# A selective scan's slots reordered: decays half a slot earlier, due work first, one step of dt a slot, and the scan's first state read as a column operand

## The chip, the cores and the metric

The kernel runs on one NeuronCore of one Trainium2 chip. The metric is the device time of that core in microseconds (us). The kernel before took 5128.9 us in the median of three runs (5122.36 to 5136.76 us). Only one core is used, so nothing waits for another core.

Five engines take part, each with its own queue that it works off strictly in order: TensorE (PE in the profile), VectorE (DVE), ScalarE (ACT), GpSimd (POOL), and SyncE (SP), which here only issues DMAs. An instruction that waits for a semaphore holds up everything behind it on its own queue.

## The reference, cut to what matters

The program is a network of four layers on two sequences (B = 2) of 1024 positions and 1024 features. The change touches only the attention half of layer 2, a selective state-space block, here shortened:

```
proj = hidden_states @ in_proj_w             # 1024 -> 2 x 2048
x, z = split(proj); x = silu(causal_conv4(x))
ssm_p = einsum('bdl,ed->ble', x, x_proj_w)   # 64 + 16 + 16 values per position
dt_r, B, C = rmsnorm of the three parts
dt = softplus(dt_r @ dt_proj_w + dt_bias)
A = -exp(A_log)
# for every channel d (2048) and state n (16), over the positions t:
h[t] = exp(dt[t] * A) * h[t-1] + dt[t] * B[t] * x[t]
y[t] = sum over n of h[t] * C[t]
out = ((y + D * x) * silu(z)) @ out_proj_w
```

## The kernel before, in words

`l2_attn(b, ...)` (from L1061) is called once for each of the two sequences, b = 0 and 1. A sequence is cut into two halves of 512 positions, u = 0 and 1 (`HALF` = 512), and the 2048 channels into 16 chunks c of 128. The second half begins where the first ended, so the last state of half 0 must reach half 1.

**A slot.** The recurrence runs in 2 * SL = 256 slots k for each sequence, 128 for each half, eight for each chunk. `of(k)` turns a slot into (u, c, q, jj). A slot holds 2 x 128 rows, a row being one channel with one state, so it has two scans, m = 0 and 1, of 128 x 512. For slot k the program issues:

- `rows(k)`, six slots early: a DMA that reads dt * x of 16 channels back from DRAM (`dxd`), each repeated for its 16 states, into a tile `h` (128 x 1024, nine buffers). L1273.
- `times_b(k)`, two slots early: GpSimd multiplies h by B. L1279.
- `decay(k, m)`: TensorE spreads dt over the states (`rep` times `hl`, L1286) into a PSUM tile, and ScalarE makes exp(A * dt) of it in place (L1288). There are eight PSUM tiles of 128 x 512 for everything, handed out as they come free.
- in half 1 only, also in `decay`: ScalarE works on one column, h[:, 0] += exp(A dt)[:, 0] * hst (L1291), so that the kept state `hst` of half 0 enters.
- `scan(k, m)`: VectorE's `tensor_tensor_scan`, decay times state plus input, with initial value 0.0. L1296.
- `keep(k)`, one slot late, in half 0 only: ScalarE copies the last column of both scans into `hst`. L1304.
- `times_c(k)`, one slot late: VectorE multiplies both scans' results by C. L1307.
- `states(k)`, in odd slots: TensorE sums over the states with `sel` into y (L1318), and once a chunk adds D * x (L1316).

**The order is written out by hand** (`manual_schedule`): the loop at the end of `l2_attn` fixes each engine's order. Into the slots it weaves other work of the block: two matmuls a slot from a list `todo` (the next half's input projection L1349, the gate's L1403, the output projection L1441), and a table `late` of work that is due in a given slot, filled by `at(k, f)`. In slot k the order is: issue rows, times_b, keep(k-1); first matmul; scan(k,0), decay(k+1,0); the due work; second matmul; scan(k,1), decay(k+1,1); states, times_c(k-1).

**Due work.** For each chunk, 16 slots ahead, `l2_dt(u, c, k)` makes dt: a matmul in slot k (L1211), then in slot k+1 three ScalarE operations (Relu, Abs, Exp: L1221 to L1223), in k+2 three more (L1226 to L1228), in k+3 two GpSimd operations (L1231, L1232), in k+4 one (L1235), in k+5 the product with x (L1238) and its four DMAs to `dxd` (L1240), in k+7 a ScalarE rounding copy into `hl` and GpSimd's remainder (L1247, L1252), in k+8 the remainder's two DMAs (L1258). x is loaded in slot k+3 (L1520's list, tile `xi`, two buffers). Other due work: the convolution for half 1 (`l2_x` on ScalarE, `l2_taps` on VectorE L1124, `l2_silu` on ScalarE L1129 with its DMA to `xcd` L1130), the gate's silu (`silu_z`, L1388; each silu costs a load of the activation table before and one after, L193), the normalisation of ssm_p (`l2_norm`, `l2_spread`), and `y_out`: ScalarE copies y out of PSUM (L1332), GpSimd multiplies it by the gate (L1333), a DMA sends it to `yd` (L1334).

The tiles `e`, `one`, `lg` and `rl` of the dt work have one buffer each; `dtx`, the product with x, uses the tile `e`, and `y_out` uses the tag `one`.

Of the kernel before, what the change touches and what calls it, by code (L numbers as in the profile page):

```python
# [27 lines left out]
class Net:  # L28
# [1032 lines left out]
    def l2_attn(self, b, ready, last):  # L1061
# [4 lines left out]
        with (  # L1066
# [56 lines left out]
                for k in range(1, 4):  # L1123
                    nc.vector.scalar_tensor_tensor(p, xp[:, k : k + HALF], cw[:, c, k : k + 1], p, ALU.mult, ALU.add)  # L1124

            def l2_silu(u, c, p):
                acc = tmp("xo")
                self.other = True
                nc.scalar.activation(acc, p, AF.Silu)  # L1129
                nc.sync.dma_start(xcd[u][c][:], acc)  # L1130
                return acc

            def l2_px(u, c, acc):
# [24 lines left out]
                    elif c % 4 < 3:  # L1158
                        quarter[-1](c % 4 - 1)

            def l2_norm(u):
# [9 lines left out]
                nc.scalar.activation(pn, p[:, : 4 * NF], AF.Square)  # L1171
                ss = self.small([P, 4, 3], "ss")
# [14 lines left out]
                return pnv  # L1187
# [20 lines left out]
            def l2_dt(u, c, k):  # L1208

                p = self.ps()  # L1210
                nc.tensor.matmul(  # L1211
                    p, wd[c // 8][: NF + 1, (c % 8) * P : (c % 8 + 1) * P], norms[u][0], start=True, stop=True
                )
                xs[u, c] = xc = tmp("xi")
                at(k + 3, nc.sync.dma_start, xc, xcd[u][c][:])
                e, one, lg = tmp("e", 1), tmp("one", 1), tmp("lg", 1)
                dt, dtx = lg, e
                rl = tmp("rl", 1)

                def act1():  # L1220
                    nc.scalar.activation(rl, p, AF.Relu)  # L1221
                    nc.scalar.activation(e, p, AF.Abs)
                    nc.scalar.activation(e, e, AF.Exp, scale=-1.0)  # L1223

                def act2():
                    nc.scalar.activation(one, e, AF.Identity, bias=self.one)  # L1226
                    nc.scalar.activation(lg, one, AF.Ln)
                    nc.scalar.activation(one, one, AF.Identity, bias=neg)  # L1228

                def pool1():  # L1230
                    nc.gpsimd.tensor_tensor(e, e, one, ALU.subtract)  # L1231
                    nc.gpsimd.tensor_tensor(lg, lg, e, ALU.add)  # L1232

                def sum1():
                    nc.gpsimd.tensor_tensor(dt, lg, rl, ALU.add)  # L1235

                def times_x():
                    nc.gpsimd.tensor_tensor(dtx, dt, xc, ALU.mult)  # L1238
                    for j in range(4):
                        nc.sync.dma_start(dxd[u][c][:, j, :], dtx[32 * j : 32 * j + 32, :])  # L1240

                low = [None]

                def parts():

                    hl[u, c] = tp.tile([P, 2, HALF], R, tag="hl", bufs=2, name=self.nm("hl"))
                    nc.scalar.copy(hl[u, c], dt.unsqueeze(1).to_broadcast([P, 2, HALF]))  # L1247

                def rest():

                    lo = low[0] = tp.tile([P, HALF], R, tag="lo", bufs=1, name=self.nm("lo"))
                    nc.gpsimd.tensor_tensor(lo, dt, hl[u, c][:, 0, :].bitcast(F), ALU.subtract)  # L1252

                def send():

                    lo = low[0]
                    for j in range(2):
                        nc.sync.dma_start(  # L1258
                            hl[u, c][64 - 64 * j : P - 64 * j, j, :].bitcast(F), lo[64 * j : 64 * j + 64, :].bitcast(F)
                        )  # L1260

                for n, f in ((1, act1), (2, act2), (3, pool1), (4, sum1), (5, times_x), (7, parts), (7, rest), (8, send)):
                    at(k + n, f)


# [17 lines left out]
            def decay(k, m):  # L1283
                u, c, q, jj = of(k)
                dA[k, m] = self.ps()
                nc.tensor.matmul(dA[k, m], rep[:, 4 * m + q, :], hl[u, c][:, jj, :], start=True, stop=True)  # L1286
                g = 16 * c + 4 * q + 2 * jj + m
                nc.scalar.activation(dA[k, m], dA[k, m], AF.Exp, scale=A[:, g : g + 1])  # L1288
                if u:
                    h0 = hs[k][:, m, 0:1]  # L1290
                    nc.scalar.activation(h0, dA[k, m][:, 0:1], AF.Identity, scale=hst[:, g : g + 1], bias=h0)  # L1291

            def scan(k, m):
                u, c, q, jj = of(k)
                g = 16 * c + 4 * q + 2 * jj + m
                nc.vector.tensor_tensor_scan(  # L1296
                    hs[k][:, m, :], dA.pop((k, m)), hs[k][:, m, :], 0.0, ALU.mult, ALU.add
                )

            def keep(k):  # L1300
# [27 lines left out]
            def y_out(k):  # L1328
                u, c = k // SL, k % SL // 8
                sz = zt.pop((u, c))  # L1330
                yo = tmp("one", 1)
                nc.scalar.copy(yo, py.pop((u, c)))  # L1332
                nc.gpsimd.tensor_tensor(sz, sz, yo, ALU.mult)  # L1333
                nc.sync.dma_start(yd[u][c][:], sz)  # L1334

            def ins(u):

                def one(u, c):
# [6 lines left out]
                    def call(k, now):  # L1345
                        if k == 0:
                            w["p"] = self.ps()
                        p = w["p"]
                        nc.tensor.matmul(  # L1349
                            p, w["w"][:, k * P : (k + 1) * P], self.xcols(k, u0, HALF), start=k == 0, stop=k == KD - 1  # L1350
                        )
                        if k == KD - 1:
                            def x():
                                w["x"] = l2_x(u, c, p)
                            at(now + 1, x)
                            at(now + 2, lambda: l2_taps(c, p, w["x"]))

                            def s():
                                w["s"] = l2_silu(u, c, p)
# [5 lines left out]
            def xproj(u):  # L1365

                def one(c2):
# [7 lines left out]
                    def call(n, now):  # L1375
                        l2_px(u, 2 * c2 + n, w["x"][:, n * HALF : (n + 1) * HALF])
                        if 2 * c2 + n == NCH - 1:
                            at(now + 1, lambda: at(now + 3, l2_spread, u, l2_norm(u)))
# [83 lines left out]
            with self.tc.manual_schedule():  # L1462
# [12 lines left out]
                take(xproj(1), 4)  # L1475
                take(z0[12:] + z1[:6], 20)
                taken = 0
                at(-BEFORE, lambda: at(4 - BEFORE, l2_spread, 0, l2_norm(0)))
                for k in range(-BEFORE, 2 * SL + 6):
                    if -16 <= k < 2 * SL - 16 and k % 8 == 0:  # L1480
                        l2_dt((k + 16) // SL, (k + 16) % SL // 8, k)
# [26 lines left out]
                        times_b(k + 2)  # L1508
                    if 0 <= k - 1 < 2 * SL:
                        keep(k - 1)  # L1510
                    pe()
                    for m in range(2):
                        if live:
                            scan(k, m)
                        if 0 <= k + 1 < 2 * SL:
                            decay(k + 1, m)
                        if m:
                            break
                        for f, args in late.pop(k, []):
                            f(*args)  # L1520
                        pe(True)
                    if k % 2 == 1 and 0 <= k - 2 < 2 * SL:
                        states(k - 2)
                    if 0 <= k - 1 < 2 * SL:
                        times_c(k - 1)
                    if live and k % 8 == 4:
                        at(k + 8, y_out, k)
                    if live and k % 8 == 0:
                        skip(k // SL, k % SL // 8)
                while late:  # L1530
# [462 lines left out]
```

## Time and profile before

| what | value |
|---|---|
| median of three runs | 5128.9 us |
| the profiled execution | 5130.32 us |
| its span, first to last instruction | 5128.4 us |
| granted TensorE clock, mean | 0.968 |
| instructions | 50257 |
| VectorE scans (L1296) | 1024, 1207 ns each, 1204.1 us |
| VectorE times_c (L1307) | 512, 1193 ns each, 610.8 us |
| GpSimd times_b (L1279) | 512, 2367 ns each, 1201.0 us |
| ScalarE exp of the decay (L1288) | 1024, 657 ns each, 667.9 us |
| ScalarE column operation (L1291) | 512, 352 ns each, 180.0 us |

The profiled execution took 5130.32 us, 1.9 us more than its span and 1.4 us more than the median of the runs; sums are made against 5130.3. The page gives each engine's busy time, a picture of the span in 40 slices of 128 us (a digit is the busy share in tenths), and groups of instructions by line, with the idle time of the engine just before them and what ended it. The waits give the same by pairs, the timeline lists instructions in order, and the busy time of a stretch is given by windows. Lines of VectorE that follow each other without a wait overlap a little: two scans together take 2.33 us, not 2.41.

### The profile page before, as it was taken

The numbers are of one execution on the slowest core, as the hardware profiler recorded it, in microseconds if no ns is written. First come the engines' busy times: TensorE is split into PE (matmuls) and PEld (weight loads), VectorE is DVE, ScalarE is ACT, GpSimd is POOL, SyncE is SP. The second block draws the span as 40 slices with busy tenths as digits, with TensorE's granted clock in tenths as the row PEclk, the third lists the DMA queues.
The fourth block names the chain that finished last, engine by engine and source line by source line (L and its number), as shares of the span: only waits on it lengthen the run. The fifth ranks groups of instructions, "written<-read, shape, count | busy, mean of one in ns | idle before, by whom it ended". The sixth has DMA issues, their size and how long they took to land. (4 is left out here: it accounts for less than half of the span.)

```text
span 5128.4 us, 50257 instructions
## 1 busy us (share of the span) xinstructions
PE 4706.3 (92%) x16584; PEld 2237.2 (44%) x16584; DVE 3128.0 (61%) x4322; ACT 2109.7 (41%) x4485; POOL 2097.7 (41%) x1259
## 2 busy tenths in 40 slices
PE   8989989998897888999999999899888988899999
PEld 3347645433332333455433576554333333344544
DVE  5453256389999997225365422652899999963153
ACT  2431232377677774001024311424776777720010
POOL 2013121078798885100020220200887998831010
PEclk9999999999999999999999999999999999999999
DMA  2144212388889998201111432113888899971100
GB/s 88 36 159 143 97 48 81 131 216 217 220 225 242 236 244 226 90 33 46 49 67 38 173 119 89 54 51 103 220 219 224 214 247 245 249 210 65 55 20 33
DMA packets 254871, 708.06 MB, mean 138 GB/s; under 512 B 37008, under 2 KB 54544, under 8 KB 254612
## 3 DMA queue, kind: packets, MB, share of 16 engines
q1 hardware_dynamic: 248340, 683.88, 46.7%
q0 software_dynamic: 6272, 20.98, 1.2%
q8 instruction: 133, 2.18, 0.2%
q14 instruction: 126, 1.03, 0.1%
HBM read 599.60 MB, written 86.25 MB: 134 GB/s over the span
## 5 line engine op out<-in xcount | busy, mean ns | idle before, releaser
L1296 DVE TENSOR_TENSOR_SCAN h<-ps,h 128x512 f32<-128x512 f32 x1024 | 1204.1, 1207 | 88.9 <-ACT h L1291 47.2
L1279 POOL TENSOR_TENSOR h<-h,br 128x1024 f32<-128x1024 f32 x512 | 1201.0, 2367 | 43.3 <-DMA h<-dxd 20.7
L1286 PE MATMUL ps<-hl,rep 128*128 128x512 f32 x1024 | 717.9, 708 | 119.9 <-DVE h L1296 94.7
L1288 ACT ACTIVATE ps<-ps,l_Alog 128x512 f32<-128x512 f32 x1024 | 667.9, 657 | 216.9 <-PE ps L1286 213.6
L1307 DVE TENSOR_TENSOR h<-h,ps 128x1024 f32<-128x1024 f32 x512 | 610.8, 1193 | 0.0
L1403 PE MATMUL ps<-xT,w 128*128 128x512 f32 x1024 | 541.1, 615 | 10.2 <-DVE h L1296 7.9
L1608 POOL TENSOR_TENSOR x<-x,row 128x1024 f32<-128x1024 f32 x48 | 112.3, 2349 | 796.0 <-PE ps L130 796.0
L1286 PEld LDWEIGHTS ps<-hl,rep 128*128 128x128 f32 x1024 | 198.6, 195 | 523.6 <-DVE h L1296 340.1
L152 DVE TENSOR_TENSOR x<-x,ps 128x512 f32<-128x512 f32 x192 | 128.4, 681 | 434.4 <-PE ps L1785 145.6
L1318 PE MATMUL ps<-h,sel 128*32 128x512 f32 x2048 | 365.1, 638 | 18.8 <-DVE h L1307 18.2
L104 PE MATMUL ps<-xT,w 128*128 128x512 f32 x768 | 336.1, 592 | 0.0
L177 ACT ACTIVATE rs<-mv 128x1 f32<-128x1 f32 (+2 forms) x88 | 17.9, 203 | 705.7 <-DVE mv L171 705.4
L1441 PE MATMUL ps<-w,w 128*128 128x512 f32 x512 | 279.9, 630 | 20.8 <-DMA w<-yd 12.1
L1403 PEld LDWEIGHTS ps<-xT,w 128*128 128x128 f32 x1024 | 190.6, 195 | 204.2 <-issue 136.7
L104 PE MATMUL ps<-w,xT 128*128 128x512 f32 (+1 forms) x768 | 278.3, 522 | 0.0
L1124 DVE SCALAR_TENSOR_TENSOR ps<-xp,l_convw,ps 128x512 f32<-128x512 f32 x192 | 144.4, 752 | 213.4 <-ACT ps L1119 208.9
L767 POOL TENSOR_TENSOR s<-s,l1r 128x512 f32<-128x512 f32 x64 | 66.5, 1040 | 487.7 <-DVE l1r L766 481.8
L1349 PE MATMUL ps<-xT,w 128*128 128x512 f32 x512 | 251.9, 602 | 0.7
L1291 ACT ACTIVATE h<-ps,h,hst 128x1 f32<-128x1 f32 x512 | 180.0, 352 | 118.5 <-POOL h L1279 93.9
L1782 PE MATMUL ps<-w,xT 128*128 128x512 f32 x512 | 227.4, 597 | 0.0
L1622 PE MATMUL ps<-w,w 128*128 128x512 f32 x512 | 222.6, 594 | 4.2 <-DMA w<-yd 4.2
L104 PEld LDWEIGHTS ps<-xT,w 128*128 128x128 f32 x768 | 144.8, 189 | 183.4 <-issue 177.6
(289 smaller groups left out, 7319.9 us busy)
## 6 DMA issues: line engine op xcount, KB each, us to landing
h<-dxd SPq DMA_DIRECT2D x512, 512.0 KB, 7.2
w<-l_in SPq DMA_DIRECT2D x128, 512.0 KB, 6.7
w<-l_out SPq DMA_DIRECT2D x96, 512.0 KB, 6.2
w<-l_conv SPq DMA_DIRECT2D x54, 512.0 KB, 3.9
w<-cvd SPq DMA_DIRECT2D x36, 512.0 KB, 3.3
w<-l_fw SPq DMA_DIRECT2D x32, 512.0 KB, 4.4
xcd<-xo SPq DMA_DIRECT2D x64, 256.0 KB, 2.2
xi<-xcd SPq DMA_DIRECT2D x64, 256.0 KB, 5.4
```

What stands on the lines that cost most here:

```text
L104: self.nc.tensor.matmul(out, lhsT, rhs, start=j == 0, stop=j == n - 1)
L1279: nc.gpsimd.tensor_tensor(hs[k], hs[k], norms[of(k)[0]][1].unsqueeze(1).to_broadcast([P, 2, HALF]), ALU.mult)
L1286: nc.tensor.matmul(dA[k, m], rep[:, 4 * m + q, :], hl[u, c][:, jj, :], start=True, stop=True)
L1288: nc.scalar.activation(dA[k, m], dA[k, m], AF.Exp, scale=A[:, g : g + 1])
L1296: nc.vector.tensor_tensor_scan(hs[k][:, m, :], dA.pop((k, m)), hs[k][:, m, :], 0.0, ALU.mult, ALU.add)
L1307: nc.vector.tensor_tensor(hs[k], hs[k], norms[of(k)[0]][3].unsqueeze(1).to_broadcast([P, 2, HALF]), ALU.mult)
L1318: nc.tensor.matmul(py[u, c][32 * j : 32 * j + 32, :], self.sel[:, q, :], hs[k - 1 + j // 2][:, j % 2, :], start=False, stop=q == 3,)
L1349: nc.tensor.matmul(p, w["w"][:, k * P : (k + 1) * P], self.xcols(k, u0, HALF), start=k == 0, stop=k == KD - 1)
L1403: nc.tensor.matmul(p, w["w"][:, k * P : (k + 1) * P], self.xcols(k, u * HALF, HALF), start=k == 0, stop=k == KD - 1)
L1441: nc.tensor.matmul(p, y[:, cc, t * P : (t + 1) * P], wt[:, cc * HALF : (cc + 1) * HALF], start=c2 == 0 and cc == 0, stop=last,)
L1622: nc.tensor.matmul(acc[tt], y[:, cc * HALF + tt * P : cc * HALF + (tt + 1) * P], w[:, cc * HALF : (cc + 1) * HALF], start=c == 0, stop=c = ...
L1782: nc.tensor.matmul(p, self.xcols(k, tt * P, P), wt[k][:, ns], start=k == 0, stop=False)
```

## The change

The edits, all within `l2_attn`:

1. The column operation of ScalarE (L1291) is gone; in half 1 the scan takes the column of `hst` as its initial value instead of 0.0.
2. In slot k the decays issued are (k+1, 1) after the first scan and (k+2, 0) after the second, instead of (k+1, 0) and (k+1, 1).
3. The due work comes ahead of the slot's matmuls and scans, just behind keep(k-1), instead of behind the first scan.
4. dt's chain has one ScalarE operation a slot from the third on and one GpSimd operation a slot, and ends in slot k+10 instead of k+8. The DMAs of the product leave one slot after it, x is loaded one slot later, and the product uses the tile `one` instead of `e`.
5. `y_out` copies y one slot earlier, into a tile of its own, GpSimd multiplies two slots later and the DMA goes one slot after that.
6. The DMA of half 1's convolution result goes one slot later, and the normalisation is split over two slots.

```
@@ l2_silu
-                nc.sync.dma_start(xcd[u][c][:], acc)
+                if u:
+                    at(now + 1, nc.sync.dma_start, xcd[u][c][:], acc)
+                else:
+                    nc.sync.dma_start(xcd[u][c][:], acc)
@@ l2_dt
-                at(k + 3, nc.sync.dma_start, xc, xcd[u][c][:])
+                at(k + 4, nc.sync.dma_start, xc, xcd[u][c][:])
-                dt, dtx = lg, e
+                dt, dtx = lg, one
...
-                for n, f in ((1, act1), (2, act2), (3, pool1), (4, sum1), (5, times_x), (7, parts), (7, rest), (8, send)):
+                for n, f in (
+                    (1, act1), (2, act2), (3, act3), (4, act4), (5, act5), (5, pool1), (6, pool2), (7, sum1),
+                    (8, times_x), (8, parts), (9, send_x), (9, rest), (10, send),
+                ):
                     at(k + n, f)
@@ decay
                 nc.scalar.activation(dA[k, m], dA[k, m], AF.Exp, scale=A[:, g : g + 1])
-                if u:
-                    h0 = hs[k][:, m, 0:1]
-                    nc.scalar.activation(h0, dA[k, m][:, 0:1], AF.Identity, scale=hst[:, g : g + 1], bias=h0)
@@ scan
-                    hs[k][:, m, :], dA.pop((k, m)), hs[k][:, m, :], 0.0, ALU.mult, ALU.add
+                    hs[k][:, m, :], dA.pop((k, m)), hs[k][:, m, :], hst[:, g : g + 1] if u else 0.0, ALU.mult, ALU.add
@@ y_out
-                yo = tmp("one", 1)
+                yo = tmp("yo", 1)
                 nc.scalar.copy(yo, py.pop((u, c)))
-                nc.gpsimd.tensor_tensor(sz, sz, yo, ALU.mult)
-                nc.sync.dma_start(yd[u][c][:], sz)
+                at(k + 9, nc.gpsimd.tensor_tensor, sz, sz, yo, ALU.mult)
+                at(k + 10, nc.sync.dma_start, yd[u][c][:], sz)
@@ the loop over the slots
+                    for f, args in late.pop(k, []):
+                        f(*args)
                     pe()
                     for m in range(2):
                         if live:
                             scan(k, m)
-                        if 0 <= k + 1 < 2 * SL:
-                            decay(k + 1, m)
+                        if 0 <= k + 1 + m < 2 * SL:
+                            decay(k + 1 + m, 1 - m)
                         if m:
                             break
-                        for f, args in late.pop(k, []):
-                            f(*args)
                         pe(True)
...
-                        at(k + 8, y_out, k)
+                        at(k + 7, y_out, k)
```

The functions act1 to act5, pool1, pool2 and send_x are the old act1, act2, pool1 and times_x taken apart, with the same operations. In `l2_norm` the first part (copy, four transposes, squares) became `l2_norm1`, called in the slot in which the whole ran before; the rest and `l2_spread` come one slot later (for half 1; for half 0 all of it stays in one slot).

More of the change, by code (lines that the diff above doesn't have):

```diff
@@ L1124, in l2_taps, with l2_silu @@
                     nc.vector.scalar_tensor_tensor(p, xp[:, k : k + HALF], cw[:, c, k : k + 1], p, ALU.mult, ALU.add)
-            def l2_silu(u, c, p):
+            def l2_silu(u, c, p, now=0):
                 acc = tmp("xo")
@@ L1159, in l2_in, with l2_norm1 @@
                         quarter[-1](c % 4 - 1)
-            def l2_norm(u):
+            def l2_norm1(u):
                 raw = tmp("xo")
@@ L1171, in l2_norm @@
                 nc.scalar.activation(pn, p[:, : 4 * NF], AF.Square)
+                return p, pn
+            def l2_norm(u, p, pn):
                 ss = self.small([P, 4, 3], "ss")
@@ L1222, in act1, with act2, act3, act4 @@
                     nc.scalar.activation(e, p, AF.Abs)
+                def act2():
                     nc.scalar.activation(e, e, AF.Exp, scale=-1.0)
-                def act2():
+                def act3():
                     nc.scalar.activation(one, e, AF.Identity, bias=self.one)
+                def act4():
                     nc.scalar.activation(lg, one, AF.Ln)
+                def act5():
                     nc.scalar.activation(one, one, AF.Identity, bias=neg)
@@ L1231, in pool1, with pool2 @@
                     nc.gpsimd.tensor_tensor(e, e, one, ALU.subtract)
+                def pool2():
                     nc.gpsimd.tensor_tensor(lg, lg, e, ALU.add)
@@ L1238, in times_x, with send_x @@
                     nc.gpsimd.tensor_tensor(dtx, dt, xc, ALU.mult)
+                def send_x():
                     for j in range(4):
@@ L1358, in s @@
                             def s():
-                                w["s"] = l2_silu(u, c, p)
+                                w["s"] = l2_silu(u, c, p, now + 3)
                                 silu_z()
@@ L1377, in call @@
                         if 2 * c2 + n == NCH - 1:
-                            at(now + 1, lambda: at(now + 3, l2_spread, u, l2_norm(u)))
+                            at(now + 1, lambda: w.update(n=l2_norm1(u)))
+                            at(now + 2, lambda: at(now + 4, l2_spread, u, l2_norm(u, *w["n"])))
                     return load, [(call, n) for n in range(2)]
@@ L1477, in l2_attn @@
                 taken = 0
-                at(-BEFORE, lambda: at(4 - BEFORE, l2_spread, 0, l2_norm(0)))
+                at(-BEFORE, lambda: at(4 - BEFORE, l2_spread, 0, l2_norm(0, *l2_norm1(0))))
                 for k in range(-BEFORE, 2 * SL + 6):
```

## The prediction

> **What bounds the kernel now.** I read the page's slices first, then busy time by windows, then VectorE's waits, then the timeline at one wait.
>
> ```profile
> DVE  5453256389999997225365422652899999963153
> ```
>
> VectorE is full in two stretches of some seven slices: the slots of sequence 0 and of sequence 1. Elsewhere TensorE leads, and the change leaves that work alone. The windows cut the stretches at the first slot of half 1 (columns: length, then busy us of PE, PEld, DVE, ACT, POOL).
>
> ```profile
> 1052.00:1532.90 480.90, 425.52 (x1334) 161.82 (x1332) 459.42 (x434) 341.56 (x655) 415.45 (x224) 0.98 0.83 220
> 1532.90:2008.00 475.10, 401.55 (x1254) 149.56 (x1255) 448.25 (x407) 342.94 (x678) 403.04 (x214) 0.95 0.93 241
> 3601.00:4080.50 479.50, 426.63 (x1336) 162.52 (x1334) 459.40 (x434) 342.08 (x655) 415.37 (x224) 0.97 0.83 220
> 4080.50:4548.00 467.50, 401.35 (x1254) 148.13 (x1252) 445.89 (x404) 343.15 (x679) 403.37 (x214) 0.95 0.93 245
> ```
>
> VectorE is busy for 1813.0 of 1903.0 us; 90.0 us of idle time is all that a better order can win. The waits say what ends it (us, times, longest).
>
> ```profile
> DVE h L1296 <- ACT h L1291: 47.2, 63, 2.3
> ...
> DVE h L1296 <- ACT ps L1288: 31.4, 28, 5.7
> ```
>
> By windows, all 47.2 us of the first row lie in halves 1 (26.1 and 21.1) and all of the second in halves 0 (13.2 and 18.1). The timeline shows such a wait in half 0 on ScalarE:
>
> ```profile
> 1100.27 0.66 ACT L1288 ACTIVATE ps<-ps,l_Alog 128x512 f32<-128x512 f32 x1 [1.53 <-PE ps L1286]
> 1100.86 0.59 ACT L1332 COPY one<-ps 128x512 f32<-128x512 f32 x1
> 1101.46 1.28 ACT L1129 ACT_TABLE_LOAD   x1
> 1102.76 0.60 ACT L1129 ACTIVATE xo<-ps 128x512 f32<-128x512 f32 x1
> 1103.25 1.14 ACT L1388 ACTIVATE zo<-zo 128x512 f32<-128x512 f32 x2
> 1104.41 1.28 ACT L193 ACT_TABLE_LOAD   x1
> 1105.70 0.66 ACT L1288 ACTIVATE ps<-ps,l_Alog 128x512 f32<-128x512 f32 x1
> ```
>
> Between the slot's two exps stand 4.9 us of due work. The second scan of the next slot could start about 1104.1 and starts at 1106.40, 2.32 us late, behind the last line.
>
> **Part by part.**
>
> *Decays half a slot sooner, due work first (edits 2, 3).* The instructions stay the same. In the slot shown, due work could start behind keep at 1098.75; 4.9 us of it and one exp of 0.66 end at 1104.3, against a scan due at about 1104.1: 0.2 us late instead of 2.3. Most other bundles are smaller and leave nothing. Of the 31.4 us one 5.7 belongs to a sequence's first scan, which stays; 25.7 remain, of which I take 5 to stay: 20.7 won. An earlier decay holds its PSUM tile longer. The built program tells which tile each decay reuses: before, 196 of 1024 take the tile of a scan that only one further scan has followed (the decay's own scan is the third after it); after, 80 decays have that distance and the others more. So the tiles are no new limit.
>
> *No column operation (edit 1).* ScalarE loses 512 x 0.352 = 180 us; that alone is worth nothing, it is 72% busy here. What counts is the 47.2 us. Going through them scan by scan, 31.9 us fall on second scans, where due work lies between the exps (as above) and 0.35 us of column operation comes on top; 15.3 us fall on first scans, where ScalarE itself waited for GpSimd's times_b. Of the first kind I take 1 us to stay. Of the second, the scan now waits for GpSimd without 0.4 us of ScalarE between, and edits 4 and 5 take stalls from GpSimd; I take 6 to stay. Won: 40.2.
>
> Against this, 512 scans now read a column. No scan of the trace does. The nearest rows are two of VectorE's with one operation, shape and mixture of PSUM and SBUF, without and with a column (`rinv`):
>
> ```profile
> L1723 DVE SCALAR_TENSOR_TENSOR x<-ps,rinv,x 128x512 f32<-128x512 f32 x32 | 22.9, 746 | 9.0 <-PE ps L104 8.7 <-issue 0.3
> ...
> L628 DVE SCALAR_TENSOR_TENSOR qkv<-cf,ps 128x512 f32<-128x512 f32 x22 | 15.1, 686 | 69.4 <-PE ps L612 69.4
> ```
>
> 746 - 686 = 60 ns. The rows L266 (a column, 751) and L454 (a copy, 687) differ by 64. The Trainium skill, "VectorE: DVE Perf Modes", section "Scalar operands", puts a constant and a column side by side with no price; by it the edit is free. Its page "ScalarE: Activation LUTs", section "What ACT_TABLE_LOAD costs", counts about 93 ns for each column operand on ScalarE. The sums: 0, 512 x 0.060 = 30.7, or 47.6 us. I take 30.7, since the rows are of the same engine and the built program encodes the scan in that same instruction class. All of it is on the path: VectorE bounds half 1. This price eats half of what the waits give, so the halves 1 gain little.
>
> *dt one step a slot, GpSimd's gate later (edits 4, 5).* No operation is added. GpSimd has eight times_b of 2.367 and six products of 1.272 per chunk: 26.6 us, 3.32 a slot. VectorE without waits needs 3.36 (times_c 1.115, scans 1.133 and 1.112 from start to start) and 3.48 with columns. So GpSimd has little room, and its stalls matter: on batch 0 it waited 24.3 us for y's copy (L1333), 17.1 for x's load (L1238), 16.3 for `hl` (L1252). Each of these now has a slot more. They are off the path while GpSimd is ahead, and I count them only in the 9.3 us taken off first scans above.
>
> The DMAs move as well. The sends of the product leave SP's queue a slot after the product, so SP no longer stands on GpSimd (85.1 us on batch 0). But their landing comes closer to two readers. The first row load of the chunk is issued in the next slot instead of five later; from there to the first scan it has six slots, 20 us, against 7.2 for landing and 2.4 for times_b. And `one` is written again by the next chunk's act3 two slots after the sends, where `e` had four: ScalarE waits for the four landings, and exps and y's copy queue behind it. SP reaches slot 9's row load 1.4 us (median) after the slot's first scan, four issues take 1.7, landing 2.9 (median; 9.4 at most): 6.0 us, and ScalarE arrives at 6.7. Nothing typically; up to 6 us in a bad case. Of these 3.3 are covered: the next scan is due 5.5 us after keep, and keep, act3, y's copy and an exp take 0.2 + 0.7 + 0.6 + 0.7 = 2.2. I take 0; a gain is excluded, since a wait is only added.
>
> *Edit 6 and the start.* The longer chain must fit the 23 slots before the first scan. TensorE streams there without gaps, and ScalarE's loads of tables, not the chain, time it; the decay for slot 0 moves earlier, the product about 5 us later. I take 0, between -3 and +3 for each sequence.
>
> **Sum.** 5130.3 - 20.7 - 40.2 + 30.7 = 5100.1 us in the profiled execution; 1.4 less, 5099 us, on the scale of the median.
>
> **Rivals.**
>
> *GpSimd paces half 1.* The 15.3 us of first-scan waits stay, now on times_b, and so do a few of the second kind that hid behind it. For: in half 1 GpSimd is at 403 of 475 us and often ends a product less than 0.5 us before its reader. Against: it loses its stalls, and the columns slow VectorE to 3.48. Time: 9 us above the sum, about 5109.
>
> *The column is free.* 5099 - 31 = 5068. For: the page's silence, and a scan takes twice as long per element as the rows compared, so a fixed load may hide. Against: two pairs of rows.
>
> *ScalarE waits for the product's landing (slower).* The place is act3, two slots behind the sends, 62 times or so. It decides once the exps become late by 0.5 us a chunk (62 x 0.5 = 31, the whole gain). At 0.8 us a chunk it costs 50: about 5149. For: DMA engines are busy for 0.93 of half 1 and landings reach 9.4. Against: the typical 6.0 us lie before ScalarE's arrival, with 3.3 us of cover behind.
>
> *The order doesn't do what it says*: waits for ScalarE only turn into waits for TensorE's decays, and gains and columns cancel: 5129.
>
> **Chances.** The sum 0.45 (its own range 5085 to 5115), GpSimd 0.17, free column 0.12, slower 0.14, no effect 0.12. A measurement tells 0.3% from no change, 15.4 us: faster is below 5113.5, slower above 5144.3. Faster: 0.40 + 0.11 + 0.12 = 0.63. Slower 0.14. Same: the rest, 0.23. The range reaches down to the free column and up to short of the slower rival: 5066 to 5142.
>
> **What would show it.** In the profile after: scans of half 1 near 1265 ns where those of half 0 stay at 1207; no row L1291; waits of scans for exps under 10 us; those for times_b under 10 us; stretches of about 470 us for halves 0 (480.2 - 10.3) and 467 for halves 1 (471.3 - 20.1 + 15.4); no wait of act3 on `dxd`. Scans unchanged in length would put the free column in its place; ScalarE idle before act3 with a DMA as the releaser, the slower rival; a first scan later than 1052 us, a chain that is too long for its start.

## The result, and the profile after

The changed kernel took 5145.3 us in the median of seven runs (5136.19 to 5151.61), against 5128.9 us for the kernel before on the same chip: a ratio of 1.0034, 95% interval 1.0021 to 1.0046. It is 16 us slower, where 30 us faster was forecast. The profiled execution took 5151.61 us at a span of 5149.9 us, 6.3 us above its median.

VectorE's busy slices read almost as before. They can't show a loss of 0.3%.

```profile
DVE  5453256389999997225364422652899999962153
```

The windows, cut at the first scan of each half, say more (columns: length, then busy us of PE, PEld, DVE, ACT, POOL).

```profile
1060.50:1542.80 482.30, 416.93 (x1332) 160.43 (x1332) 462.49 (x435) 335.91 (x652) 412.60 (x223) 0.95 0.83 216
1542.80:2012.40 469.60, 396.43 (x1238) 143.21 (x1238) 452.27 (x398) 260.18 (x418) 402.34 (x215) 0.94 0.91 242
3620.50:4096.10 475.60, 413.13 (x1332) 159.35 (x1332) 460.06 (x436) 335.92 (x652) 412.64 (x223) 0.96 0.84 219
4096.10:4566.40 470.30, 398.86 (x1238) 144.07 (x1238) 452.21 (x398) 260.26 (x418) 402.30 (x215) 0.93 0.89 242
```

With the same cut the kernel before has 484.3, 467.0, 482.3 and 461.2 us. So halves 0 gained 8.7 us and halves 1 lost 11.7. The first scan of a sequence also comes later: 67.0 us behind the transposes of the normalisation instead of 62.8. Together the two blocks of layer 2 are 11.5 us longer. The profiled runs differ by 10 us more outside the block, which the change does not touch.

The groups show what the scans cost and wait for.

```profile
L1313 DVE TENSOR_TENSOR_SCAN h<-ps,hst,h 128x512 f32<-128x512 f32 x512 | 629.5, 1267 | 35.3 <-ACT ps L1308 35.3
L1313 DVE TENSOR_TENSOR_SCAN h<-ps,h 128x512 f32<-128x512 f32 x512 | 600.1, 1208 | 29.5 <-ACT ps L1308 28.8
```

A scan with a column takes 1267 - 1208 = 59 ns more, as forecast. But scans still wait 64.1 us for exps, where the sum left 12 us for all waits of scans. ScalarE's waits name the reason, and SP's waits stand beside it (us, times, longest):

```profile
ACT one L1235 <- DMA dxd<-one: 187.5, 57, 9.9
```

```profile
SPq L1293 <- PE ps L1335: 702.0, 191, 13.3
```

act3 (L1235), which writes `one` for the next chunk, waits 57 times for the product that still leaves the same tile. 50 of the 64 us of scan waits fall in the slot right behind these stops. SP waits 702 us at row loads (L1293) for buffers of `h` that TensorE's sums (L1335) free. Before it was less:

```profile
SPq L1273 <- PE ps L1318: 528.8, 186, 8.4
```

Two chunks of sequence 1 show how the two meet. Each line begins with start and length in us. In the first chunk, an ordinary one, slot 9 begins with a scan at 4072.58. SP's part of the timeline comes first, then ScalarE's.

```profile
4067.57 8.30 SPq L1293 DMA_DIRECT2D h<-dxd  x2
4075.97 1.94 SPq L1257 DMA_DIRECT2D dxd<-one  x4
```

```profile
4078.44 0.58 ACT L1349 COPY yo<-ps 128x512 f32<-128x512 f32 x1
4080.99 0.72 ACT L1235 ACTIVATE one<-e,one 128x512 f32<-128x512 f32 x1 [1.97 <-DMA dxd<-one]
4081.61 0.64 ACT L1308 ACTIVATE ps<-ps,l_Alog 128x512 f32<-128x512 f32 x1
```

SP is through with its row loads at 4075.9, sends the product 3.4 us after the slot's first scan, and is done with the four sends at 4077.9. ScalarE comes to act3 at 4079.0 and stands until 4081.0. The exp behind it still comes in time: no scan waits here.

In the second chunk slot 9 begins at 4184.94. SP, ScalarE and VectorE:

```profile
4191.12 0.81 SPq L80 DMA_DIRECT2D w<-l_in  x2
4192.03 0.53 SPq L1293 DMA_DIRECT2D h<-dxd  x1
4192.87 3.72 SPq L1257 DMA_DIRECT2D dxd<-one  x4
```

```profile
4202.44 0.72 ACT L1235 ACTIVATE one<-e,one 128x512 f32<-128x512 f32 x1 [9.91 <-DMA dxd<-one]
4203.07 1.22 ACT L1308 ACTIVATE ps<-ps,l_Alog 128x512 f32<-128x512 f32 x2
```

```profile
4203.74 1.28 DVE L1313 TENSOR_TENSOR_SCAN h<-ps,hst,h 128x512 f32<-128x512 f32 x1 [7.08 <-ACT ps L1308]
```

Loads of weights (L80) and the row load stand ahead of the sends, which go 7.9 us after the slot's first scan. act3 stands 9.9 us, the exps queue behind it, and VectorE loses 7.1 us. The loss is made in such chunks: 19 of 60 stops are longer than 3.3 us, and behind these 19 the scans wait 45.7 us; behind the other 41 they wait 4.9 us.

### The profile page after: what moved, and what is told of

It is laid out like the page before. It is cut to its first block, busy times and chain, and to the rows that moved or that the text cites. A ratio compares the mean times of both kernels' runs of the same rounds, so it can differ in the third digit from the quotient of the medians.

```text
span 5149.9 us, 49284 instructions
## 1 busy us (share of the span) xinstructions
PE 4695.5 (91%) x16584; PEld 2226.1 (43%) x16584; DVE 3153.8 (61%) x4322; ACT 1940.2 (38%) x3973; POOL 2094.2 (41%) x1259
## 5 line engine op out<-in xcount | busy, mean ns | idle before, releaser
L1306 PE MATMUL ps<-hl,rep 128*128 128x512 f32 x1024 | 699.9, 689 | 171.0 <-DVE h L1313 151.3
L1313 DVE TENSOR_TENSOR_SCAN h<-ps,hst,h 128x512 f32<-128x512 f32 x512 | 629.5, 1267 | 35.3 <-ACT ps L1308 35.3
L1313 DVE TENSOR_TENSOR_SCAN h<-ps,h 128x512 f32<-128x512 f32 x512 | 600.1, 1208 | 29.5 <-ACT ps L1308 28.8
L1324 DVE TENSOR_TENSOR h<-h,ps 128x1024 f32<-128x1024 f32 x512 | 611.9, 1195 | 1.5 <-ACT hst L1321 1.5
L1335 PE MATMUL ps<-h,sel 128*32 128x512 f32 x2048 | 327.7, 653 | 8.7 <-DVE h L1324 8.5
L1459 PE MATMUL ps<-w,w 128*128 128x512 f32 x512 | 276.0, 623 | 5.3 <-DVE h L1313 4.5
L767 POOL TENSOR_TENSOR s<-s,l1r 128x512 f32<-128x512 f32 x64 | 66.4, 1039 | 488.2 <-DVE l1r L766 482.3
L1244 POOL TENSOR_TENSOR e<-e,one 128x512 f32<-128x512 f32 x64 | 81.5, 1274 | 415.9 <-ACT one L1241 415.2
```

The costliest lines, as they stand in the source:

```text
L1313: nc.vector.tensor_tensor_scan(hs[k][:, m, :], dA.pop((k, m)), hs[k][:, m, :], hst[:, g : g + 1] if u else 0.0, ALU.mult, ALU.add)
L1324: nc.vector.tensor_tensor(hs[k], hs[k], norms[of(k)[0]][3].unsqueeze(1).to_broadcast([P, 2, HALF]), ALU.mult)
L1335: nc.tensor.matmul(py[u, c][32 * j : 32 * j + 32, :], self.sel[:, q, :], hs[k - 1 + j // 2][:, j % 2, :], start=False, stop=q == 3,)
L1459: nc.tensor.matmul(p, y[:, cc, t * P : (t + 1) * P], wt[:, cc * HALF : (cc + 1) * HALF], start=c2 == 0 and cc == 0, stop=last,)
```

## The experiments

All are compared with the kernel before, run on the same chip beside them; two variants are compared by their ratios, since they ran on four chips. "Uncertain by" is half the width of a 95% interval. Theories 1 and 2 are those (T1, T2) of the text quoted with each run.

**A tile of its own for the product.** `pn` of the normalisation shares the tag `cr`, to make room.

```
-                dt, dtx = lg, one
+                dt, dtx = lg, tmp("dtx", 1)
```

> The kernel after, with the product dt*x in a tile of its own, so that act3 no longer waits for the four landings (room for it comes from letting the norm's squares share a tile with C's rows). Theory one (the landings hold up ScalarE, and with it the exps): the 187 us of ScalarE's idle time before act3 go, and some 45 of the 64 us in which scans wait for exps go with it: about 5100 us against 5145 after and 5129 before. Theory two (act3 is only where the delay shows, and rows, GpSimd or TensorE's PSUM tiles hold the slots anyway): the waits come back on the next of these, 5135 us or more.

Measured: 5104.3 us, ratio 0.9962 (0.9948 to 0.9976). From 1.0034 this is 37 us less, and act3's wait is gone. SP still stands at the chunk's first row load for the landing:

```profile
SPq L1293 <- DMA dxd<-dtx: 196.5, 64, 8.0
```

That stop has six slots of lead, and scans of this kernel wait for GpSimd's products 0.7 us in all. Theory 1 holds.

**ScalarE's column operation back** (edit 1 undone, the shared tile kept).

```
+                if u:
+                    h0 = hs[k][:, m, 0:1]
+                    nc.scalar.activation(h0, dA[k, m][:, 0:1], AF.Identity, scale=hst[:, g : g + 1], bias=h0)
...
-... hst[:, g : g + 1] if u else 0.0, ...
+... 0.0, ...
```

> The kernel after, with ScalarE's column operation back behind each exp of half 1 and the initial value 0.0 in the scans; all else as after. Theory one (the column costs VectorE 59 ns in 512 scans, 30 us on the path): scans of half 1 return to 1208 ns, the column operation brings some waits for GpSimd back: 5120 to 5135 us. Theory two (the column is paid for by what it frees): ScalarE now waits for times_b half a slot sooner than before the change, and the time is 5145 us or more.

Measured: 5138.9 us, ratio 1.0025 (1.0014 to 1.0036), between the two. All scans take 1205 ns, but they wait for the column operation again:

```profile
DVE h L1316 <- ACT h L1311: 67.4, 22, 8.8
```

act3 still waits 143.8 us. The column costs VectorE 30 us, and without it the kernel is only 5 us faster (uncertain by 9): its absence costs nearly as much on ScalarE.

**Due work behind the first scan again** (edit 3 undone, the shared tile kept).

```
-                    for f, args in late.pop(k, []):
-                        f(*args)
                     pe()
...
                         if m:
                             break
+                        for f, args in late.pop(k, []):
+                            f(*args)
                         pe(True)
```

> The kernel after, with the due work back behind the slot's first scan and decay; all else as after. Theory one (due work first puts the convolution's taps ahead of the first scan, which starts 4 us later in each sequence, but takes bundles out from between the exps): the first scan comes 4 us earlier, waits for exps behind bundles come back at 10 to 20 us: 5145 to 5160 us. Theory two (due work first is itself the loss): 5135 us or less.

Measured: 5145.2 us, ratio 1.0040 (1.0025 to 1.0056), no better than the changed kernel. Its first scan comes 5 us sooner, and ScalarE's waits at act3 fall to 94.0 us. In exchange `times_c` (L1324) waits for `keep` (L1321), 1.5 us in the changed kernel:

```profile
DVE h L1324 <- ACT hst L1321: 33.2, 27, 3.5
```

**Edit 1 alone**, on the kernel before: ScalarE's column operation (the three lines added above) taken out there, and in the scan

```
-... 0.0, ...
+... hst[:, g : g + 1] if u else 0.0, ...
```

> The kernel before, with edit 1 alone: the scans of half 1 read the kept state as a column, and ScalarE's column operation is gone. Theory one: 30 us on VectorE against some 35 of the 47 us of waits for the column operation: 5120 to 5130 us. Theory two (the waits come back on exps and times_b): 5140 to 5160 us.

Measured: 5123.4 us, ratio 0.9994 (0.9984 to 1.0004). The price of 30 us and the end of most waits before scans of half 1 (8.3 us are left) almost cancel. The column is no cause of the loss.

**The first slot mended.** In the own-tile kernel the due work of slot 0 alone stands behind the first scan.

```
-                    for f, args in late.pop(k, []):
-                        f(*args)
+                    if k:
+                        for f, args in late.pop(k, []):
+                            f(*args)
...
                             scan(k, m)
+                        for f, args in late.pop(k, []):
+                            f(*args)
```

> The changed kernel with the product in a tile of its own, and in the first slot of each sequence only, the due work stands behind the first scan instead of ahead of it. T1 (with due work first, three taps of 2.3 us stand ahead of the very first scan, about 4 us a sequence with what waits for them): about 8 us under the own-tile kernel, near 5096, and the way from the norms' transposes to the first scan back at 63 us instead of 67. T2 (the later start comes from the longer chain of dt): no change from the own-tile kernel, about 5104, first scan still 67 us behind the transposes.

Measured: 5104.0 us, ratio 0.9947 (0.9934 to 0.9960), and 62.8 us from transposes to first scan in both sequences. The way is mended as theory 1 says. Against own tile, the ratio falls by 0.0015, which an uncertainty of 0.0019 does not tell from nothing, so the same edit was made on the changed kernel as well:

> The changed kernel with only the first slot of each sequence mended: there the due work stands behind the first scan again. The shared tile and act3's stall stay. T1 (the start is a term of its own, 4.3 us a sequence from transposes to first scan): 6 to 9 us under the changed kernel, 5136 to 5140. T2 (it is given back at once, since what is held up then stands in front of the second scan): within 3 us of the changed kernel.

Measured: 5137.5 us, ratio 1.0017 (1.0008 to 1.0025), 8.7 us less than the changed kernel (uncertain by 7.7), and 4.1 and 4.2 us less on the way to the first scan. The timeline of the changed kernel shows what stands there:

```profile
1058.25 2.34 DVE L1124 SCALAR_TENSOR_TENSOR ps<-xp,l_convw,ps 128x512 f32<-128x512 f32 x3 [7.67 <-ACT ps L1119]
...
1060.50 2.33 DVE L1313 TENSOR_TENSOR_SCAN h<-ps,h 128x512 f32<-128x512 f32 x2
```

Three taps of the convolution, due in slot 0, wait for ScalarE's `l2_x` and then hold up a first scan that needs neither. Moving dt's chain was not needed to mend it.

**The column's price doubled.** In the own-tile kernel, scans of half 0 read a column of zeros as well.

```
-... hst[:, g : g + 1] if u else 0.0, ...
+... hst[:, g : g + 1] if u else zero, ...
```

> The own-tile kernel with the scans of half 0 reading a column of zeros as well: the column's price doubled, nothing moved. T1 (59 ns a scan, all of it on VectorE's path): scans of half 0 at 1264 instead of 1205 ns, 512 x 0.059 = 30 us over the own-tile kernel, near 5135, and the two halves 0 longer by 15 each. T2 (in half 0 the longer scans eat waits, 14.9 us before scans and others): 10 to 20 us over it, 5114 to 5124.

Measured: 5141.8 us, ratio 1.0026 (1.0015 to 1.0038), 33 us over own tile (uncertain by 9). From start to start, a scan follows a scan in 1194 ns instead of 1133, and `times_c` a scan in 1175 instead of 1115. All of the price is on the path.

**The column operation on ScalarE, but early.** Own tile and mended start; the scans start from 0.0, and ScalarE's two column operations for slot k+1 stand behind slot k's decays.

```
+            def h0(k):
+                u, c, q, jj = of(k)
+                for m in range(2):
+                    g = 16 * c + 4 * q + 2 * jj + m
+                    x = hs[k][:, m, 0:1]
+                    nc.scalar.activation(x, dA[k, m][:, 0:1], AF.Identity, scale=hst[:, g : g + 1], bias=x)
...
+                    if SL <= k + 1 < 2 * SL:
+                        h0(k + 1)
```

> As the kernel with own tile and mended start, but the scans of half 1 start from a constant again, and ScalarE's two column operations for slot k+1 stand at the end of slot k, behind both decays of that slot, where the product with B should have ended. T1 (the column costs 30 us on VectorE, and ScalarE has room for 180 us of column operations if it takes them early): all scans near 1206 ns, some 20 to 30 us under own tile with mended start, near 5070. T2 (ScalarE waits there for GpSimd's product with B, and holds up the exps behind it, which stand half a slot ahead only): the won 30 us come back as waits of scans for exps, 5095 or more.

Measured: 5124.2 us, ratio 0.9987 (0.9976 to 0.9997), 21 us over the kernel with the column on VectorE. The scans of half 1 are back at 1210 ns, and wait:

```profile
DVE h L1320 <- ACT h L1315: 36.9, 34, 3.0
DVE h L1320 <- POOL h L1299: 23.3, 12, 3.6
DVE h L1320 <- ACT ps L1308: 22.6, 18, 5.7
```

The time is as theory 2 has it, but not its mechanism: in this trace the column operation (L1315) never waits for GpSimd. It stands behind the exp of a slot later, and that exp waits for TensorE:

```profile
1618.28 0.66 ACT L1308 ACTIVATE ps<-ps,l_Alog 128x512 f32<-128x512 f32 x1 [1.47 <-PE ps L1306]
1618.87 0.59 ACT L1315 ACTIVATE h<-ps,h,hst 128x1 f32<-128x1 f32 x2
```

The scan behind these lines starts 1.76 us late. Other scans wait for GpSimd's products (23.3 us): with 3.36 us a slot for VectorE, GpSimd's 3.32 has no lead.

**Edit 3 undone** in the own-tile kernel, by the same lines as in the changed kernel above.

> The own-tile kernel with the due work behind the slot's first scan again, between the two decays (edit 3 undone alone). T1 (due work first is worth its place in the steady slots, once act3 doesn't stand waiting): scans wait again some 10 to 15 us more for exps behind bundles, less the 8 us of the start won back: 5100 to 5112. T2 (with the decays half a slot sooner, the place of the due work is worth nothing and only costs the start): 8 us under own tile, near 5096.

Measured: 5124.4 us, ratio 0.9997 (0.9985 to 1.0010), above either range. Against the kernel with own tile and mended start, whose first slot has the same order, it is 26 us more (uncertain by 9). The halves 0 take 490 and 488 us instead of 474 and 470, and the wait is one that no theory named:

```profile
DVE h L1324 <- ACT hst L1321: 33.7, 28, 3.5
```

Due work behind a slot's first scan delays `keep` (L1321) in the next, and `times_c` (L1324) overwrites what `keep` must read first. In the kernel before, with its due work in the same place but the older order of decays, `times_c` never waited (L1307, 0.0 us).

**Edit 2 undone** in the kernel with own tile and mended start.

```
-                        if 0 <= k + 1 + m < 2 * SL:
-                            decay(k + 1 + m, 1 - m)
+                        if 0 <= k + 1 < 2 * SL:
+                            decay(k + 1, m)
```

> The kernel with own tile and mended start, with the decays of a slot both made in the slot before it, as in the kernel before (edit 2 undone alone). T1 (a bundle of due work of 4.9 us is longer than a slot, and only the half slot of lead covers the rest): each large bundle makes the next slot's first scan late by about 2 us, some 12 of them in each half 0: 20 to 40 us over own tile with mended start, 5125 to 5145. T2 (due work first alone is enough, since a slot's exps are then in a row): within 8 us of it, 5100 to 5112.

Measured: 5115.4 us, ratio 0.9979 (0.9969 to 0.9988), 16 us more (uncertain by 8): less than theory 1 had, more than theory 2. The scans' waits rise from 36.6 to 56 us.

**Edits 4 and 5 undone** in the same kernel: the old slots of dt's chain with the product in `e`, and GpSimd's gate right behind y's copy.

```
-                    (1, act1), (2, act2), (3, act3), (4, act4), (5, act5), (5, pool1), (6, pool2), (7, sum1),
-                    (8, times_x), (8, parts), (9, send_x), (9, rest), (10, send),
+                    (1, act1), (1, act2), (2, act3), (2, act4), (2, act5), (3, pool1), (3, pool2), (4, sum1),
+                    (5, times_x), (5, send_x), (7, parts), (7, rest), (8, send),
```

> The kernel with own tile and mended start, with dt's chain in the slots of the kernel before (all of its ScalarE steps in two slots, product and sends in the same slot, product in e) and GpSimd's gate right behind y's copy (edits 4 and 5 undone). T1 (with due work ahead of the exps, larger bundles on ScalarE and GpSimd's stalls behind them make exps and products late): 10 to 30 us over own tile with mended start, 5115 to 5135. T2 (edits 4 and 5 move only what lies beside VectorE): within 8 us of it, 5096 to 5112.

Measured: 5123.1 us, ratio 0.9990 (0.9979 to 1.0000), 22 us more (uncertain by 9), in the range of theory 1. In its profile halves 0 take 482.4 and 479.8 us instead of 473.9 and 469.9, and halves 1 are a little shorter. The waits of its scans are hardly longer in all (38.0 instead of 36.6 us), and VectorE's idle time in halves 0 rises by 10 us, some half of the difference; so the gain is shown, and how it comes about is not.

**act3 one slot later**, in the changed kernel with the shared tile.

```
-                    (1, act1), (2, act2), (3, act3), (4, act4), (5, act5), (5, pool1), (6, pool2), (7, sum1),
+                    (1, act1), (2, act2), (4, act3), (5, act4), (5, act5), (5, pool1), (6, pool2), (7, sum1),
```

> The changed kernel with one number moved: dt's step that writes the sum with one again, act3, stands a slot later, together with the logarithm, so that the sends of the product before have three slots to land instead of two. The product stays in the shared tile. T1 (the loss is that landing): of the 57 waits of 187.5 us before act3 only what exceeds one slot of 3.7 us stays, 34.5 us in 14 chunks by the list of waits, most of the gain of the own tile comes back: 5105 to 5120. T2 (the own tile won by something else, such as its place or one write less on the tile): no less than 5135.

Measured: 5123.6 us, ratio 0.9992 (0.9982 to 1.0002), 22 us less than the changed kernel and nearer to theory 1, though above its range; 85.5 us of the wait stay where 35 were expected:

```profile
ACT one L1235 <- DMA dxd<-one: 85.5, 30, 9.3
```

More room helps; a fixed landing time does not explain what stays, since the last send goes up to 13 us behind the slot's first scan.

**dt's rounding copy one slot later** in the kernel with own tile and mended start, where ScalarE stands 76.0 us at this copy.

```
-                    (8, times_x), (8, parts), (9, send_x), (9, rest), (10, send),
+                    (8, times_x), (9, parts), (9, send_x), (10, rest), (11, send),
```

> The kernel with own tile and mended start, with the rounding copy of dt (parts) one slot later, its rest and its sends too: ScalarE stands at this copy for GpSimd's sum, 76.0 us in 47 chunks in that kernel, where the copy follows the sum by one slot (by three in the kernel before). T1 (in half 1 these stands make exps late: 7 or 8 waits of scans at the slot behind, some 6 us a sequence): 5 to 12 us less, 5092 to 5099. T2 (they end before an exp is due, or the rest on GpSimd then holds up the logarithm's next write of the same tile): 5100 to 5110.

Measured: 5133.9 us, ratio 1.0008 (0.9997 to 1.0020), 31 us more. Both theories miss. ScalarE's stand of 76.0 us is gone, but at the other end of the chain TensorE's decays now wait for the landing of the remainder in `hl` (22.8 us in 11 waits before this edit):

```profile
PE ps L1306 <- DMA hl<-lo: 61.6, 25, 6.4
```

The chain has no slot to give.

**The sends ahead of the row load**, in the changed kernel with the shared tile and act3 in its slot: `send_x` moves from the list of due work to the front of slot 9.

```
+                early[k + 9] = send_x
...
+                    if k in early:
+                        early.pop(k)()
                     if 0 <= k + 6 < 2 * SL:
                         rows(k + 6)
```

> The changed kernel with one thing moved: in slot 9 of a chunk the four sends of the product stand ahead of that slot's row load on SP's queue instead of behind it. Product, tile and act3 stay. T1 (half of the stall is SP's: its row load is issued 2.85 us after the slot's first scan where the prediction had 1.4, the load itself takes another 0.6, and only then the sends go): the sends go at about 0.5 to 1.5 us, and of the 187.5 us of act3's waits (median 2.5, 58 times) only the excess over 2 to 3 us stays, 50 to 80 us; time 5115 to 5130. T2 (the landing takes what it takes, about 4 us from the last send in the median and 6 to 10 in the dense stretches, and SP's place matters little, or SP then stands on GpSimd's product): over 5135.

Measured: 5108.5 us, ratio 0.9962 (0.9948 to 0.9977): the whole 37 us, without a tile more, better than theory 1 had. Its waits, and SP in the chunk shown above, whose slot 9 here begins at 4043.41:

```profile
ACT one L1235 <- DMA dxd<-one: 37.1, 13, 6.9
```

```profile
4043.73 1.72 SPq L1257 DMA_DIRECT2D dxd<-one  x4
4046.20 1.22 SPq L1294 DMA_DIRECT2D h<-dxd  x2
```

The sends go 0.3 us after the slot's first scan instead of 3.4, and act3 does not wait. The slot's row load is no later than before: in both kernels it goes 2.8 us after that scan. The scans' waits fall from 64.1 to 26.9 us. What stays of act3's wait lies where loads of weights still stand ahead of the sends or the landing is long; five stops of 4.7 to 6.9 us keep scans waiting for 13.2 us.

**Both and the mended start.** Own tile, mended start, sends first.

> The kernel with own tile and mended start, with the sends ahead of the slot's row load. T1 (with the tile of its own nobody waits for the landing but the chunk's first row load, one slot behind the sends, and SP stands there 196 us in 64 chunks, which GpSimd's products partly see as 71 us of waits for rows): earlier sends free SP earlier, GpSimd's waits for rows fall below 50 us, 0 to 6 us less than own tile with mended start, 5097 to 5104. T2 (SP stands on GpSimd's product instead): 5104 to 5112.

Measured: 5089.8 us, ratio 0.9931 (0.9915 to 0.9947), the best of all, about 35 us under the kernel before and 53 under the changed one. It is 8 us under the kernel with own tile and mended start, more than theory 1 had, but the uncertainty is 11. GpSimd waits less for rows, as theory 1 says (35.3 instead of 71.1 us), and the waits of decays for `hl` end (0.4 us instead of 22.8), which it had not said:

```profile
POOL h L1300 <- DMA h<-dxd: 35.3, 25, 4.6
```

```profile
L1314 DVE TENSOR_TENSOR_SCAN h<-ps,hst,h 128x512 f32<-128x512 f32 x512 | 629.6, 1272 | 4.9 <-ACT ps L1309 4.9
L1314 DVE TENSOR_TENSOR_SCAN h<-ps,h 128x512 f32<-128x512 f32 x512 | 599.7, 1209 | 22.8 <-ACT ps L1309 21.5
```

11 us of the last row are the first scans of the two sequences.

## Why the prediction was wrong

The rival "ScalarE waits for the product's landing", put at 0.14 and 5149 us, is what happened, with the sign that the prediction had named for it: ScalarE idle before act3, and a DMA that ends the wait.

**The step that failed** is the one on act3's wait: sends and landing done at 1.4 + 1.7 + 2.9 = 6.0 us after the slot's first scan, ScalarE there at 6.7, "I take 0". The traces have, as medians over the 58 of 60 chunks in which act3 stands in the changed kernel (57 of these stops end with a landing):

| us after slot 9's first scan | forecast | changed kernel | sends first |
|---|---|---|---|
| SP at the slot's row load | 1.4 | 2.85 | - |
| first send | 1.4 | 3.5 | 0.2 |
| last send | 3.1 | 5.0 | 1.6 |
| ScalarE at act3 | 6.7 | 6.9 | 6.8 |
| act3 starts | 6.7 | 9.7 | 7.4 |

The issues (1.5 us) and ScalarE's arrival were right. SP was wrong twice. The 1.4 us was read in the trace of before, as the time at which SP reached the row load, and the sends stand behind that load: its own issue, about 0.6 us, was left out. And SP reaches the load later, 2.85 us: at the loads of slot 9 alone it waits 294.8 us for TensorE to free `h`, where it waited 118.4 before. Together that makes the first send 2.1 us later. The landing is the other part: where act3 waits, it starts 3.9 us (median) after the last send, not 2.9. From 6.0 us these two lead to 9.1 and, less 0.2 for the issues, to 8.9; the measured 9.7 is above that, as medians don't add. The typical wait this makes is 2.5 us, and the cover of 3.3 us does carry it. What it does not carry is the tail, up to 9.9 us where the prediction had 6 in a bad case and still took 0: the 19 stops above the cover make 45.7 us of scan waits. So the term was reckoned from medians and lost in the tail. With the first send 3.3 us earlier and the same tile (sends_first) 13.2 us of scan waits behind act3 stay of 50. In time the term is 37 us (uncertain by 10), by two edits that share nothing else.

That the rival's 5149 us lies so near the measured 5145 is in part luck: it had 50 us for this wait where it is 37, and the start, which it did not have, makes up for most of the difference.

**The start** was taken at 0 and is 8.3 us (4.1 + 4.2 by the traces). The prediction looked at the chain's length there, and said that a first scan later than 1052 us would show a chain too long; it came at 1060.5, but the cause is edit 3, which puts the taps ahead of the first scan. (4.2 of the 8.4 us by which it is later were there before the transposes of the normalisation.) That check would have misled.

These two explain 37 + 8.3 of the 46 us between 5099 and 5145. With both taken out, the own-tile kernel with mended start has a ratio of 0.9947, 5102 us on the scale of before, near the sum. That does not make every other term right. Edits 4 and 5 gained some 22 us for which the sum had no term, so the other terms together must have given less than forecast, and that the two balance is luck:

- *The column*, 30.7 us: 512 x 59 ns = 30.2 by the groups, about 33 by doubling it. Right, and the rival "free" is out. The prediction weighed a page of the Trainium skill ("VectorE: DVE Perf Modes", section "Scalar operands") that gives no price; the measured 59 ns decides.
- *Edit 1's waits*, -40.2 us: alone it nets -3 us (uncertain by 5), so against a price of 30 its waits give some 33 where only it is made. The 40.2 counted on edits 2 to 5 too.
- *Edits 2 and 3*, -20.7 us: undoing edit 2 costs 16 us and undoing edit 3 costs 26. The two sizes are not to be added, since each is measured with the other in place. That they help is shown. For edit 2 the scans' waits show it; what edit 3 takes away, with edit 2 in place, is not the forecast wait for exps but that of `times_c` for `keep`.
- *Edits 4 and 5*, no term of their own: undoing them costs 22 us (uncertain by 9), in halves 0. Here the prediction missed a gain: it called the stalls off the path. The mechanism stays open.
- *GpSimd as the pace of half 1*: not in the changed kernel, where no scan waits for its products; it appears once the column leaves VectorE (own_h0_late, 23.3 us).
- *The stretches*: 470 and 467 us were forecast, with another cut, so their sum is compared: 937. The changed kernel has 948.9 in the mean of the two sequences, own tile with mended start 931.2.

## What to carry to other kernels

When a step is moved, reckon the queue that must issue its DMAs from that queue's place in the new order, with the instruction ahead of it included: a time read in the old order is that of another slot. Reckon it by the worst chunks as well as by the median: here the cover carried the median stop, and the whole gain was lost in a third of the chunks. A tile that serves a DMA as its source is busy until the landing (57 stops and 187.5 us here); either give it a tile of its own, or put the sends ahead of whatever the queue may have to wait for. And "due work first" is right in the steady state and wrong in the first slot, where something else is due.

## What the runs showed that was not expected

In some kernels VectorE's scans were recorded longer in full stretches: up to 1351 ns as the mean of 16 scans with a column (act3_later), where the own-tile kernel had 1261 to 1268, and times_c up to 1264 ns instead of 1190 to 1196. The starts did not move: a scan still followed a scan by 1193 ns in the median. A recorded duration here is not a rate; the distance from start to start is.

The waits of ScalarE do not move the time one for one; those of VectorE's scans do so here. Ending the 187.5 us of stops at act3 took the scans' waits from 64.1 to 25.1 us (own tile) and 26.9 us (sends first), and the time fell by 37 us in both. Removing 76.0 us of ScalarE's stand at the rounding copy cost 31 us.
